# Cross-attention block on one core: the first group's s3, T3 and s2 on VectorE, T2's own sums in the first group's last product

## The chip, the cores and the metric

One core of a Trainium2 chip runs the whole block in one launch. The time is device microseconds (us) of that core. A profile is one execution recorded by the hardware profiler; its engines are PE (TensorE's matmuls; PEld its weight loads), DVE (VectorE), ACT (ScalarE), POOL (GpSimd) and SP (SyncE, which here only issues DMAs). PE, DVE, ACT, POOL and SP each work through a queue of their own in order and wait for each other through semaphores.

## The reference

Everything is float32. With x of 8 x 256 tokens by 512, and as many tokens of context:

```python
q = layer_norm(x, ln1_w, ln1_b) @ q_w + q_b          # 16 heads of 32
k, v = ctx @ k_w + k_b, ctx @ v_w + v_b
out = softmax(mask(q @ k.T / sqrt(32))) @ v
hidden = out @ cproj_w + cproj_b + x
y = gelu(layer_norm(hidden, ln2_w, ln2_b) @ fc_w + fc_b)   # 512 -> 2048
return hidden + y @ proj_w + proj_b                        # 2048 -> 512
```

## The kernel before

The 2048 tokens are four groups (`g` = 0 to 3) of 512. Attention comes first for all groups; the change lies behind it, in the loop over `g` from line 1194, which does fc, gelu and proj for one group at a time. At its start all operands of fc lie in SBUF or in DRAM; `proj_w` is loaded during group 0.

Matrix products are made by the Winograd form of Strassen's scheme: both operands are cut into quarters "11", "12", "21", "22", and seven products of sums of quarters stand in for eight. The table `B_SUMS` (line 209) gives the right operand's sums, t1 = 12 - 11, t2 = 22 - t1, 12 = 22 - 12 (in place), t4 = 21 - t2; `A_SUMS` the left operand's s1 to s4.

**fc.** `product(k, ...)` for k = 0 to 6 makes the seven products of the outer level. Each is again cut into seven, the calls of `sub`, so a product is 7 x 8 = 56 matmul records and a group's fc is 392. `sub(n, ...)` writes PSUM bank n. The order within one product is: bank 1, copied by ACT to u1; bank 6, which DVE adds to u1, giving u2; bank 7, added to u2, giving u3; bank 5 ("22"); then bank 1 is added to a second time, then bank 7 a second time, then bank 5's second tile. So u3 must have been read from bank 7 before PE writes there again, five `sub`s into the product, and the next product's third `sub` needs bank 7 empty. DVE empties banks by adds with one operand in PSUM; GpSimd, which here works on SBUF only, adds the results into the blocks of `h`. In products 3 and 4 DVE also takes pieces of the next group's layer norm statistics (`norm_piece`), and at the start of each product, in group 1 alone, pieces of `proj_w`'s own sums (`some_p2`, lines 1318, 1319). A product ends by issuing the load of its weights for the next group (`load_w2`) on SP.

**gelu.** ACT applies it to the blocks of `h`; those of "21" and "22" during product 6, those of "12" behind it.

**proj, outer level.** `proj_w`'s quarters lie in `pw`; four sums are made from them in place in group 0 by the generator `sum_pw` on DVE, four pieces each, in this order: T3 (in "12"), T2 ("t2"), T1 ("t1"), T4 ("t4"). `some_pw(4)` makes one such sum; the four calls stand at lines 1368, 1484, 1507 and 1545. On the other side `sum_h` makes s3 = 11 - 21, s2 = 22 - s3 (in "21"), s1 = 21 + 11 (in "11") and s4 = 12 - 21 (in "12"), again four pieces each; in group 0 all of them on GpSimd, in the later groups s3, s2 and s1 on DVE and s4 on GpSimd (`deep` is true from group 1 on). In group 0 `proj(bank, a, w, ...)` issues 32 matmul records a time, in the order 11 x 11 (bank 1, which DVE then reads into u1 with `proj_b` added), s3 x T3 (bank 7), 12 x 21 (added to bank 1), s2 x T2 (bank 6), s1 x T1 (bank 5), s4 x 22, 22 x T4 (added to bank 7). Between them PE transposes the next group's tokens (`turn_next`), and DVE and GpSimd add the results and the bias (`bias_ht`, two adds on GpSimd) to the tile `ht`. Behind the last but one product DVE makes the sums of the next group's y (`y_sums`, then `split_y`), which the next group's product 0 reads.

**proj, inner level.** From group 1 on, four of these seven products (12 x 21, s2 x T2, s1 x T1, s4 x 22) are cut once more (`deep_proj`). That needs `B_SUMS` of the weights "21", T2, T1 and "22" themselves, four pieces each (`p2_sums`): three results lie in one of two places of the tile `p2` (place 0 for T2 and "22", place 3 for T1 and "21"), the third sum goes in place into `pw`, and behind the fourth piece SP stores the place to DRAM (`p2_dram`, 768 KB). T1's are made in group 0. The others are made in group 1: "22" on DVE in products 0 to 2, "21" on GpSimd, two pieces behind product 1 and two behind product 2, and T2's on DVE in products 4 to 6, over "22". From then on `p2_load` brings each back from DRAM before it is used; the order of use in a group is "21", T2, T1, "22".

Of the kernel before, what the change touches and what calls it, by code (L numbers as in the profile page):

```python
# [22 lines left out]
def tile_xattn_block(  # L23
# [299 lines left out]
    with ExitStack() as att:  # L323
# [460 lines left out]
        V, GP = nc.vector, nc.gpsimd  # L784
# [175 lines left out]
        g = 1  # L960
        begin(g, 6, 1, load_res, 0, *QUARTERS)
        begin(g, 7, 1, bias_res, 0)
        g = 2
# [6 lines left out]
        g = NG - 1  # L970
# [24 lines left out]
        def run(pieces):  # L995
            for p in pieces:
                p()
# [25 lines left out]
        k, q, v, tx = project_qk(0, "kT"), project_qk(0, "qT"), project_v(0), turn_x(0)  # L1023
# [77 lines left out]
    with ExitStack() as mlp:  # L1101
# [68 lines left out]
        def p2_sums(n, eng=V):  # L1170
            x = pw_blocks(n)
            for i in range(4):
                sum_up(eng, x, B_SUMS, i)
                if i == 3:
                    nc.sync.dma_start(p2_dram[n], p2_place(n))
                yield

        p2_late = {n: p2_sums(n, e) for n, e in (("22", V), ("21", GP), ("t2", V))}

        def some_p2(n, pieces):  # L1180
            for _ in zip(range(pieces), p2_late[n]):
                pass

        def p2_load(n):
            nc.sync.dma_start(p2_place(n), p2_dram[n])

        def some_pw(n):
            for f in zip(range(n), pw_sums):
                pass
# [4 lines left out]
        for g in range(NG):  # L1194
# [18 lines left out]
            def sum_h(which, q, eng=GP):  # L1213

                x = {n: h[n][:, :, 2 * q : 2 * q + 2, :] for n in h}
                to, a, b, op = {
                    "s3": ("s3", "11", "21", ALU.subtract),
                    "s2": ("21", "22", "s3", ALU.subtract),
                    "s1": ("11", "21", "11", ALU.add),
                    "s4": ("12", "12", "21", ALU.subtract),  # L1220
                }[which]
                add(eng, x[to], x[a], x[b], op)
# [7 lines left out]
            def norm_piece():  # L1230

                if g + 1 < NG:
                    if not norm:
                        norm.append(layer_norm(hids[g + 1], f"m{g + 1}", nc.scalar))
                        seen, roots, _ = norm[0]
                        norm.extend([*seen, *roots])
                    norm.pop(1)()
# [6 lines left out]
            def bias_ht():  # L1244

                for b, bias in ((0, projb[:, :HD2]), (1, pbd)):
                    o = out_quarter(b, 0)
                    add(GP, o, o, by_tiles(bias))
# [24 lines left out]
            def product(k, *sums):  # L1273


                wt, yn = w2[g, k], QI[FC_ORDER[k][1]]
                bank = {}

                def y_of(n):
                    if n in QUARTERS:  # L1280
                        return ys[g].t[:, yn, int(n[0]) - 1, ts(int(n[1]) - 1, P)]
                    return y2s[g][:, ("t1", "t2", "t4").index(n), yn, :]

                def sub(n, w, b, first, last):
                    if first:
                        bank[n] = bank_of(n, f"pf{n}_{k}").rearrange("p i (j s) -> p (i j) s", j=2)
                    for m in range(HF // 2):
                        mm(
                            bank[n][:, m, :],
                            wt[:, QI[w], ts(m, P)],  # L1290
                            y_of(b),
                            first and m == 0,
                            last,
                        )

                def u(n):
                    return us(n, f"u{n}_{k}").rearrange("p i (j s) -> p (i j) s", j=2)

                def made(cd, n, x):
                    some_gelus()  # L1300
                    if k in (3, 4) and cd != "22":
                        norm_piece()
                    if sums[0][1] is None:
                        add(V, block(sums[0][0], cd), bank[n], x)
                        return

                    r = h["s3"][:, parts[0] % 4 // 2, parts[0] % 2 * HF // 2 :][:, : HF // 2]
                    parts[0] += 1
                    add(V, r, bank[n], x)
                    for to, base in sums:  # L1310
                        add(GP, block(to, cd), block(base, cd), r)

                sub(1, "11", "11", True, False)
                u1 = u(1)
                nc.scalar.copy(u1, bank[1])  # L1315
                if g == 1:

                    some_p2("22", (2, 1, 1, 0, 0, 0, 0)[k])
                    some_p2("t2", (0, 0, 0, 0, 1, 1, 2)[k])
                sub(6, "s2", "t2", True, True)  # L1320
                u2 = u(2)
                add(V, u2, bank[6], u1)
                some_gelus()
                sub(7, "s3", "12", True, False)
                u3 = u(3)
                add(V, u3, bank[7], u2)
                some_gelus()
                sub(5, "21", "t1", True, False)
                made("22", 5, u3)
                sub(1, "12", "21", False, True)  # L1330
                some_gelus()
                for to, base in sums:
                    if base:
                        add(V, block(to, "11"), bank[1], block(base, "11"))
                    else:
                        nc.scalar.copy(block(to, "11"), bank[1])
                sub(7, "22", "t4", False, True)
                made("21", 7, u2)
                sub(5, "s4", "22", False, True)
                made("12", 5, u2)  # L1340
                load_w2(w2_place[g, k])
# [3 lines left out]
            load_next()  # L1345
            product(1, ("11", "21"))
            if g == 1:
                some_p2("21", 2)
            gelu("11", 0)
            ht = residual(work, hid_dram[g], "resm", f"resm_{g}")  # L1350
            product(2, ("21", "21"))
            if g == 1:
                some_p2("21", 2)
            product(3, ("12", "21"))
            if g == 0:
                load_pw("11", "12", "22")
# [3 lines left out]
            if g == 0:  # L1360
                load_pw("21")
            product(5, ("21", "21"))
            norm_piece()
            gelu("21", 0)
            gelu("22", 1)
            product(6, ("12", "12"))
            norm_piece()
            some_pw(4)
            some_gelus(len(gelus))
            gelu("12", 1)  # L1370
            deep = g > 0
            for which in ("s3", "s2"):
                for q in range(NQF):
                    sum_h(which, q, V if deep else GP)
            if not deep:
                bias_ht()

            bank = {n: bank_of(n, f"py{n}") for n in ((1, 7) if deep else (1, 7, 6, 5))}

# [25 lines left out]
            def o_add(eng, b, k, x):  # L1405
                o = out_quarter(b, k)
                add(eng, o, x, o)
# [93 lines left out]
                sum_h("s4", q)  # L1501
            if deep:
                o_add(GP, 0, 0, as_tiles(hsum[:, 4]))
                bias_ht()
            turn_next(2)
            turn_next(3)
            some_pw(4)
# [20 lines left out]
            if deep:  # L1528
                x_s4, pieces = h_blocks("12", hsum[:, 0], hsum[:, 1], hsum[:, 3])
                run(pieces[:1])  # L1530
                deep_proj(
                    x_s1, "t1", free(3), pieces[1:2], pieces[2:3], pieces[3:], y_sums[:1], y_sums[1:2]
                )
                if g + 1 < NG:
                    p2_load("21")
                for b in range(2):
                    o_add(GP, b, 1, as_tiles(free(3)))
                add_us()
                deep_proj(x_s4, "22", free(0), (), (), y_sums[2:3], y_sums[3:])
                if g + 1 < NG:  # L1540
                    p2_load("t2")
                o_add(V if g + 1 == NG else GP, 0, 1, as_tiles(free(0)))
            else:
                add_us()
                some_pw(4)
                proj(bank[5], "11", "t1", True, True)
                o_add(V, 0, 1, bank[5])
                o_add(V, 1, 1, bank[5])
                for _ in p2_sums("t1"):
                    pass  # L1550
                run(y_sums)
                bank[3] = bank_of(1, "py3")
                proj(bank[3], "12", "22", True, True)
                o_add(V, 0, 1, bank[3])
            store(0)
            if g + 1 < NG:
                y2 = wpool.tile([P, 3, 7, P], F32, tag="y2", bufs=1, name=f"y2_{g + 1}")
                split_y(g + 1, y2, 0, 1, 2, 3)
                proj(bank[7], "22", "t4", False, True)
                o_add(V, 1, 0, bank[7])  # L1560
                store(1)
            else:

                store(1, slice(HD2, D))
                for i in range(2):
                    proj(bank[7], "22", "t4", False, True, (i,))
                    o = ht[:, 2 + i, :HD2]
                    add(V, o, last_7[1] if i else bank[7][:, 0, :], o)
                    store(1, slice(HD2), (i,))
# [41 lines left out]
```

## Time and profile before

| | |
|---|---|
| median of 3 runs (lowest, highest) | 722.44 us (722.06, 723.33) |
| profiled execution, its span | 723.32 us, 721.5 us |
| granted TensorE clock | 1.00 throughout |
| PE busy | 712.7 us (99%) |
| DVE busy | 504.9 us (70%) |
| POOL busy | 486.1 us (67%) |
| ACT busy | 327.8 us (45%) |
| mean DMA rate over the span | 208 GB/s |

PE's records can be read as stages: its first fc matmul of group 0 starts at 348.53 us, group 0's proj at 392.31, group 1's fc at 442.98 and its proj at 489.07, group 2's fc at 536.55 and its proj at 580.33, group 3's fc at 627.81. The rest, up to 348.53, is the attention part. Matmuls are pipelined, so a row's length includes the tail of its last matmul, and the pace is read from start to start.

### The profile page before, as it was taken

The numbers are of one execution on the slowest core, as the hardware profiler recorded it, in microseconds if no ns is written. First come the engines' busy times: TensorE is split into PE (matmuls) and PEld (weight loads), VectorE is DVE, ScalarE is ACT, GpSimd is POOL, SyncE is SP. The second block draws the span as 40 slices with busy tenths as digits, with TensorE's granted clock in tenths as the row PEclk, the third lists the DMA queues.
The fourth block names the chain that finished last, engine by engine and source line by source line (L and its number), as shares of the span: only waits on it lengthen the run. The fifth ranks groups of instructions, "written<-read, shape, count | busy, mean of one in ns | idle before, by whom it ended". The sixth has DMA issues, their size and how long they took to land.

```text
span 721.5 us, 14867 instructions
## 1 busy us (share of the span) xinstructions
PE 712.7 (99%) x5397; PEld 630.9 (87%) x5397; DVE 504.9 (70%) x1204; ACT 327.8 (45%) x928; POOL 486.1 (67%) x430
## 2 busy tenths in 40 slices
PE   8999999999999999999999999999999999999998
PEld 7878877877887777777999889988999999999997
DVE  3676765674557556887678597799776897766972
ACT  2267788766866787872034300217103072030500
POOL 3758799987786999886559960882554835547253
PEclk9999999999999999999999999999999999999999
DMA  9516646687739785942699603995248942475021
GB/s 292 193 60 182 246 157 224 195 310 264 230 118 291 270 267 201 380 131 87 216 404 371 235 1 113 378 372 203 88 147 327 326 178 89 145 264 204 2 88 59
DMA packets 77401, 149.90 MB, mean 208 GB/s; under 512 B 7140, under 2 KB 45328, under 8 KB 74640
## 3 DMA queue, kind: packets, MB, share of 16 engines
q1 hardware_dynamic: 77072, 148.92, 58.7%
q8 instruction: 43, 0.70, 0.4%
q14 instruction: 30, 0.25, 0.1%
q0 software_dynamic: 256, 0.02, 0.0%
HBM read 112.22 MB, written 36.70 MB: 206 GB/s over the span
## 4 chain that ended last, share of the span: by engine, by line
PE 87%; DVE 3%; DMA 2%; ACT 2%; POOL 2%; issue 2%; SPq 0%; DVEq 0%; ACTq 0%; POOLq 0%
PE pf L1119 18%; PE py L1119 12%; PE ppt L699 8%; PE pv L441 7%; PE pqT L441 7%; PE po L441 6%; PE pd_t L1119 5%; PE pd L1119 5%; PE pkT L441 5%; PE s L646 5%; PE av L715 5%; PE pkT L538 2%; POOL h L1122 2%; ACT h L1259 2%; DMA pw<-in_L_xattn_proj_w_dram 2%
## 5 line engine op out<-in xcount | busy, mean ns | idle before, releaser
L1119 PE MATMUL pf<-y,w 128*128 128x128 f32 x1568 | 176.5, 276 | 1.5 <-DVE u L1122 1.5
L1119 PEld LDWEIGHTS pf<-y,w 128*128 128x128 f32 x1568 | 175.9, 192 | 2.3 <-DVE u L1122 2.1
L1122 POOL TENSOR_TENSOR h<-h,hs 128x512 f32<-128x512 f32 x88 | 113.7, 1314 | 89.4 <-DVE hs L1122 88.8
L688 POOL TENSOR_TENSOR pr<-pr,rsum 128x512 f32<-128x512 f32 x128 | 129.5, 1044 | 36.0 <-DVE rsum L686 23.8
L674 ACT ACTIVATE pr<-pr,nmax 128x256 f32<-128x256 f32 x256 | 127.7, 502 | 35.3 <-DVE nmax L664 35.2
L664 DVE CUSTOM_DVE_ANT_0 pr<-s,mb 128x256 f32<-128x256 f32 x256 | 93.6, 413 | 39.7 <-PE s L646 28.0
L1315 ACT COPY u<-pf 128x512 f32<-128x512 f32 x28 | 16.4, 585 | 164.8 <-PE pf L1119 164.8
L699 PEld LDWEIGHTS ppt<-ident,pr 128*128 128x128 f32 x512 | 57.3, 140 | 14.9 <-issue 5.2
L699 PE MATMUL ppt<-ident,pr 128*128 128x128 f32 x512 | 68.8, 277 | 0.3
L1122 DVE TENSOR_TENSOR hs<-pf,u 128x512 f32<-128x512 f32 x72 | 49.5, 688 | 12.4 <-PE pf L1119 10.8
L1259 ACT ACTIVATE h<-h,cols 128x256 f32<-128x256 f32 x128 | 52.0, 494 | 12.0 <-POOL h L1122 12.0
L1122 POOL TENSOR_TENSOR h<-h,h 128x512 f32<-128x512 f32 x20 | 27.5, 1398 | 42.9 <-DVE hs L1122 13.4
L1122 DVE TENSOR_TENSOR u<-pf,u 128x512 f32<-128x512 f32 x56 | 38.7, 690 | 25.0 <-PE pf L1119 21.3
L704 ACT COPY pt<-ppt 128x512 f32<-128x512 f32 x96 | 51.8, 573 | 7.1 <-PE ppt L699 7.1
L441 PE MATMUL pv<-vw,ctxT 128*128 128x256 f32 x224 | 52.4, 381 | 0.0
L441 PE MATMUL pqT<-xnT,qw 128*128 128x256 f32 x224 | 51.0, 380 | 0.0
L674 ACT ACTIVATION_READ_ACCUMULATOR pr<-pr,nmax 128x1 f32 x256 | 48.8, 190 | 0.0
L441 PEld LDWEIGHTS pqT<-xnT,qw 128*128 128x128 f32 x224 | 41.5, 191 | 4.9
L441 PEld LDWEIGHTS pv<-vw,ctxT 128*128 128x128 f32 x224 | 41.1, 191 | 5.3 <-issue 0.3
L1119 PE MATMUL py<-pw,h 128*128 128x256 f32 x192 | 42.4, 380 | 0.0
L1119 PE MATMUL py<-pw_t,h 128*128 128x256 f32 x192 | 42.3, 380 | 0.0
L1119 PEld LDWEIGHTS py<-pw_t,h 128*128 128x128 f32 x192 | 36.2, 190 | 4.7
(212 smaller groups left out, 1292.1 us busy)
## 6 DMA issues: line engine op xcount, KB each, us to landing
w<-w_dram SPq DMA_DIRECT2D x16, 1792.0 KB, 9.3
w<-in_L_xattn_fc_w_dram SPq DMA_DIRECT2D x36, 256.0 KB, 6.3
w<-w_dram SPq DMA_DIRECT2D x12, 768.0 KB, 7.6
ctx<-in_ctx_dram SPq DMA_DIRECT2D x16, 256.0 KB, 4.9
x<-in_x_dram SPq DMA_DIRECT2D x16, 256.0 KB, 4.5
v_dram<-st_v SPq DMA_DIRECT2D x16, 256.0 KB, 2.2
v<-v_dram SPq DMA_DIRECT2D x16, 256.0 KB, 4.6
resx<-in_x_dram SPq DMA_DIRECT2D x16, 256.0 KB, 4.6
```

The costliest lines, as they stand in the source:

```text
L441: nc.tensor.matmul(bank[n][:, i, :], l[:, c, ts(i, P)], r[:, c, :], start=first and i == 0 and c == 0, stop=last and c == HC - 1, skip_gro ...
L646: nc.tensor.matmul(banks[j][:, i, :], qT[j * HD : (j + 1) * HD, b * S + i * P : b * S + (i + 1) * P], kT[j * HD : (j + 1) * HD, b * SK : ( ...
L664: nc.vector.tensor_tensor_reduce(pr[:, j, i, :], banks[j][:, i, :], mbias[g][1][:, b, :], scale=-SCALE, scalar=FLT_MAX, op0=ALU.add, op1=A ...
L674: nc.scalar.activation(pr[:, j, i, :], pr[:, j, i, :], AF.Exp, bias=nmax[:, j, i : i + 1], scale=-1.0, accum_out=sums[:, j, i : i + 1],)
L688: nc.gpsimd.tensor_tensor(pr[:, j], pr[:, j], rsum[:, j, :, None].to_broadcast([P, NQ, SK]), ALU.mult,)
L699: nc.tensor.transpose(ps[:, kc, ts(i, P)], probs[n][:, j, i, ts(kc, P)], ident)
L704: nc.scalar.copy(pt, ps)
L715: nc.tensor.matmul(av[j * HD : (j + 1) * HD, :], vs[g, hg][:, b * NK + kc, ts(j, HD)], pts[n, j][:, kc, :], start=(kc == 0), stop=(kc == N ...
L1119: nc.tensor.matmul(ps, lhsT, rhs, start=first, stop=last, skip_group_check=True)
L1122: eng.tensor_tensor(to, a, b, op)
L1259: nc.scalar.activation(h[n][:, :, p, :], h[n][:, :, p, :], AF.Gelu_apprx_tanh, bias=col(c_fcb, half * HF + p), scale=1.0,)
L1315: nc.scalar.copy(u1, bank[1])
```

## The change

In group 0, s3 and s2 are made by VectorE like those of the later groups, and T3 is made between the two, where it was ahead of both. The bias adds of group 0 on GpSimd move from in front of the first product of proj to behind s4, where they are in the other groups.

T2's own sums are made in group 0, on VectorE, between `split_y` and the last product, and stored to DRAM; the next group's y sums go ahead of T1's own sums there. In group 1, VectorE makes the own sums of "21", one piece in each of products 0 to 3, and GpSimd those of "22", at the points where it made those of "21". Behind product 5 SP issues the load of T2's own sums from DRAM over "22".

```diff
-        p2_late = {n: p2_sums(n, e) for n, e in (("22", V), ("21", GP), ("t2", V))}
+        p2_late = {n: p2_sums(n, e) for n, e in (("21", V), ("22", GP))}
...
                 if g == 1:
-
-                    some_p2("22", (2, 1, 1, 0, 0, 0, 0)[k])
-                    some_p2("t2", (0, 0, 0, 0, 1, 1, 2)[k])
+                    some_p2("21", (1, 1, 1, 1, 0, 0, 0)[k])
                 sub(6, "s2", "t2", True, True)
...
             product(1, ("11", "21"))
             if g == 1:
-                some_p2("21", 2)
+                some_p2("22", 2)
...
             product(2, ("21", "21"))
             if g == 1:
-                some_p2("21", 2)
+                some_p2("22", 2)
...
             product(5, ("21", "21"))
+            if g == 1:
+                p2_load("t2")
             norm_piece()
             gelu("21", 0)
             gelu("22", 1)
             product(6, ("12", "12"))
             norm_piece()
-            some_pw(4)
             some_gelus(len(gelus))
             gelu("12", 1)
             deep = g > 0
             for which in ("s3", "s2"):
                 for q in range(NQF):
-                    sum_h(which, q, V if deep else GP)
-            if not deep:
-                bias_ht()
+                    sum_h(which, q, V)
+                if which == "s3":
+                    some_pw(4)
...
             if deep:
                 o_add(GP, 0, 0, as_tiles(hsum[:, 4]))
-                bias_ht()
+            bias_ht()
...
                 o_add(V, 1, 1, bank[5])
+                run(y_sums)
                 for _ in p2_sums("t1"):
                     pass
-                run(y_sums)
...
                 split_y(g + 1, y2, 0, 1, 2, 3)
+                if not deep:
+                    for _ in p2_sums("t2"):
+                        pass
                 proj(bank[7], "22", "t4", False, True)
```

## The prediction

> **What bounds the kernel.** The page's first table gives PE 99% of the span, so I looked only for PE's losses. The table of busy time by stage comes first, cut at PE's own borders: the fc products of groups 1 and 2 (numbers from zero), which issue the same 392 matmuls.
>
> ```profile
> 442.98:489.07 46.09, 44.56 (x393) 43.99 (x392) 38.61 (x58) 10.16 (x22) 31.33 (x25) 1.00 0.85 317
> 536.55:580.33 43.78, 43.78 (x394) 43.77 (x392) 31.44 (x50) 10.57 (x23) 25.00 (x21) 1.00 0.83 303
> ```
>
> The first number is the length: 46.09 against 43.78, at the same clock of 1.00, so group 1 loses 2.31 us. Group 2 needs exactly 392 x 0.1117 us. PE's timeline says where:
>
> ```profile
> 399.21 2.75 PE L1119 MATMUL py<-pw,hs 128*128 128x256 f32 x12
> 402.27 4.58 PE L1119 MATMUL py<-pw,hs 128*128 128x256 f32 x20 [0.30 <-POOL hs L1122]
> 406.69 1.04 PE L274 MATMUL pyt<-ident,hm 128*128 128x128 f32 x8
> 442.98 29.64 PE L1119 MATMUL pf<-y,w 128*128 128x128 f32 x264
> 473.31 6.52 PE L1119 MATMUL pf<-y,w 128*128 128x128 f32 x56 [0.70 <-DVE u L1122]
> 480.14 6.52 PE L1119 MATMUL pf<-y,w 128*128 128x128 f32 x56 [0.31 <-DVE u L1122]
> 487.18 2.05 PE L1119 MATMUL pf<-y,w 128*128 128x128 f32 x16 [0.52 <-DVE u L1122]
> ```
>
> Rows: start, length, engine, count, and in brackets the idle time and its releaser. Group 1 stops once in each of products 4, 5 and 6 (a product is 6.25 us, so product 4 starts at 468.0), always for a VectorE add that empties a bank. Group 0 stops once: 399.21 to 406.69 is 7.48 us for 32 matmuls that take 6.90 elsewhere (392.31 to 399.21), a loss of 0.58. **Together 2.89 us can be had**, and nothing else near the change costs PE time.
>
> **Why VectorE is late in group 1.** Its timeline in products 4 to 6, only the lines of T2's own sums and the bank adds behind them:
>
> ```profile
> 470.25 1.61 DVE L219 TENSOR_TENSOR p<-pw_t 128x512 f32<-128x512 f32 x1 [0.35 <-DMA p_dram<-p]
> 471.79 1.47 DVE L1122 TENSOR_TENSOR u<-pf,u 128x512 f32<-128x512 f32 x2
> 478.01 0.68 DVE L219 TENSOR_TENSOR p<-pw_t,p 128x512 f32<-128x512 f32 x1
> 482.91 1.15 DVE L219 TENSOR_TENSOR pw_t<-pw_t 128x512 f32<-128x512 f32 x1
> 483.98 1.75 DVE L219 TENSOR_TENSOR p<-pw_t,p 128x512 f32<-128x512 f32 x1
> ```
>
> The first even waits for the store of "22" to leave the same place. Then u2 and u3 run at 471.79 to 473.26, and PE needs bank 7 free at 468.0 + 5 x 0.893 = 472.5. The four cost 0.68 to 1.75 us each, short alone and long beside GpSimd.
>
> **Part 1: T2's sums leave products 4 to 6.** What is left there on VectorE is what group 2 has, which loses nothing. Gain 2.31. Bounds: GpSimd's backlog from its four sums could keep part of it; it stands idle 2.91 us before its run of nine adds at 474.23, so it has caught up, and I take the whole. If not, at worst nothing comes (rival B).
>
> **Part 2: the first group's s3, T3, s2 on VectorE.** Now GpSimd makes s3 beside T3 on VectorE, and both are slowed. Group 2 shows the same s3 and s2 on VectorE:
>
> ```profile
> 393.67 5.72 DVE L1122 TENSOR_TENSOR pw<-pw,pw 128x512 f32<-128x512 f32 x4
> 400.02 6.09 DVE L1122 TENSOR_TENSOR pw_t<-pw,pw 128x512 f32<-128x512 f32 x4
> 395.44 6.78 POOL L1122 TENSOR_TENSOR hs<-h,h 128x512 f32<-128x512 f32 x4
> 402.18 6.29 POOL L1122 TENSOR_TENSOR h<-h,hs 128x512 f32<-128x512 f32 x4
> 581.79 3.55 DVE L1122 TENSOR_TENSOR hs<-h,h 128x512 f32<-128x512 f32 x4
> 585.26 2.49 DVE L1122 TENSOR_TENSOR h<-h,hs 128x512 f32<-128x512 f32 x4
> ```
>
> VectorE is free at 393.75, when the gelus of "21" (8 x 0.404 us from 389.72) are done. s3: 3.55, plus 0.54 because GpSimd's last adds overlap it to 395.48 here and only 1.19 us there: 4.1 (at most T3's 5.72). T3: GpSimd has nothing to run before s2's first piece, so 2.49 (at most 5.72). It ends at 400.3; PE wants its last piece at 399.21 + 12 x 0.2156 = 401.8. The 0.58 stall goes; at both upper ends T3 would end at 405.2 and PE lose 3.4.
>
> s2 follows: one piece 0.62, then three beside GpSimd's s1, which s2 releases, at T2's 6.09 / 4 = 1.52: 5.2 (0.62 to 1.75 a piece: 2.5 to 5.9). Behind it waits u1, 0.69, now 406.2 in place of 400.1. PE needs u1 before it adds to bank 1 again, at 407.56 - 0.58 = 407.0: cover 0.8, at the upper end 0.1. T2's pieces (needed at 414.8) start after 406.2 and end by 412.3. GpSimd's s1 and s4 move ahead by some 4 us; the two bias adds (1.26 each) go behind s4, before the adds of u2 and u3 at 423.23, where GpSimd now waits 0.70. Cost nothing; without that cover they would delay those adds by 2.5.
>
> A rule that speaks against this: the Trainium skill, "SBUF — State Buffer", section "Who interferes with whom", says that a VectorE operation with two SBUF inputs and a GpSimd one that reads SBUF exclude each other for a whole instruction. By that rule each shared piece costs an estimated 0.62 + 1.26 = 1.88, u1 ends at 407.3, and the time would be about 0.3 longer, 719.9. The rows above agree that both suffer but stay under it (1.43 to 1.70).
>
> **Part 3: T2's sums in group 0's last product.** VectorE's lines there:
>
> ```profile
> 433.17 2.69 DVE L219 TENSOR_TENSOR y<-y 128x512 f32<-128x512 f32 x4
> 440.01 1.08 DVE L307 TENSOR_TENSOR y<-y,y 128x896 f32<-128x896 f32 x1
> 443.25 0.69 DVE L1122 TENSOR_TENSOR resm<-py,resm 128x512 f32<-128x512 f32 x1 [2.15 <-PE py L1119]
> ```
>
> The 2.15 us of idle time ahead of the last add is the room. T1's four sums took 430.64 to 433.17, 2.53, with GpSimd idle, as it is here (nothing after 427.85). All 0.58 earlier: split_y ends at 440.5, the sums at 443.05 (7.0 if each took 1.75: 447.5), the add 0.69 later at 443.75. Product 0 wants its bank 7 two subproducts in, at 442.40 + 1.79 = 444.2. Cover 0.45, so I cost it nothing; at the upper end 4.0.
>
> **Part 4: queues.** VectorE's "21" takes the places of "22" in products 0 to 2 (one piece less in product 0), and one piece in product 3, where VectorE waits 1.09 us for PE: even at 1.75 u3 ends at 465.8, PE needs it at 466.2. GpSimd's four sums only change their block. On SP T2's store moves from 485.76 to about 443, ahead of group 0's last output stores and of the weight load at 449.4, which wait for later events; T1's store moves from 433.28 to 435.3. "21"'s first sum at 443.8 overwrites T1's place: that store landed in 3.2 us, so 438.5 (the slowest such store took 12.8: 448.1, and PE would lose 3.0). GpSimd's first sum (457.9) overwrites T2's place: landed by 446 to 456. The added reload, 768 KB, goes out near 483, behind product 5's weights; such reloads land in 4.2 to 4.5 us, and T2 is used at 510.89 - 2.89 = 508. Hidden, with over 10 us to spare even at 12.8.
>
> **Sum.** The profiled execution took 723.32 (span 721.54, 1.8 around it), 0.88 above the median of the three runs. 723.32 - 2.31 - 0.58 = 720.43 for it; taken off the median, 722.44 - 2.89 = **719.55**. The three runs spread from -0.38 to +0.89, so the case's own range is 718.9 to 720.4.
>
> **Rivals.** A: u1 is late in group 0 (pieces of s2 at 1.75 or more, or GpSimd's adds dragging on), and the 0.58 is spent again: 720.1. For: cover of 0.8 only. Against: no row of four shared pieces averages over 1.52 on VectorE. Chance 0.07.
>
> B: PE's stops in products 4 to 6 stay, since others (GpSimd, the statistics pieces) hold VectorE back; only 0.58 comes: 721.9. Against: group 2 has all of these and none of the stops. Chance 0.12, T1's late store and a part of the stops moved to product 3 counted here, since they end in the same place.
>
> C, slower: all twelve pieces from s3 to s2 run at T3's present 1.43, because VectorE is what slows itself there. 393.75 + 17.2 + 0.69 = 411.6 against 407.0: PE loses 4.6, 724.2. It decides from a mean piece of 1.29 on, where the loss of 2.9 eats the gain; I count on (4.1 + 2.49 + 5.2) / 12 = 0.98. For: T3's own row. Against: GpSimd's s3 beside it is the work that goes. Chance 0.08.
>
> My forecast has 0.73. A measurement of this kernel can tell about 0.2% (1.4 us) from no change: forecast and A are faster (0.80), B the same (0.12), C slower (0.08). The range reaches towards B: 718.9 to 721.4.
>
> **What would show it.** Group 1's fc stage at 43.8 us, group 0 from 392.31 to its end at 50.1, no stop of PE between; T3 at some 2.5 us; u1 before 407; the last add of group 0 right behind T2's sums. Wrong if PE stops at bank 1 near 407, at bank 7 near 444, or in products 0 to 3 of group 1.

## The result, and the profile after

Six runs of the kernel after gave a median of 719.55 us (719.12 to 720.14), six of the kernel before on the same chip 722.22 (722.06 to 723.33): a ratio of 0.9961, interval 0.9949 to 0.9974, so 1.9 to 3.7 us faster. 719.55 had been forecast.

The stages of PE in the kernel after, group 0's proj and group 1's fc (start and end, length, then busy time and count of instructions of PE, PEld, DVE, ACT and POOL, clock, DMA share, GB/s):

```profile
391.31:441.41 50.10, 50.10 (x242) 44.23 (x241) 42.56 (x50) 12.69 (x26) 23.68 (x15) 1.00 0.38 145
441.41:485.18 43.77, 43.77 (x393) 43.77 (x392) 35.57 (x56) 10.56 (x23) 30.68 (x25) 1.00 0.91 349
```

They took 50.67 and 46.09 before: 0.57 and 2.32 shorter, the two amounts of the forecast (0.58 and 2.31). PE's timeline no longer has a break in either; s3 x T3 and all of group 1's fc are one row each:

```profile
398.22 7.07 PE L1119 MATMUL py<-pw,hs 128*128 128x256 f32 x32
441.41 43.93 PE L1119 MATMUL pf<-y,w 128*128 128x128 f32 x392
```

VectorE behind product 6 of group 0, with GpSimd's s1 (start, length, engine, count):

```profile
392.76 3.55 DVE L1122 TENSOR_TENSOR hs<-h,h 128x512 f32<-128x512 f32 x4
396.24 2.48 DVE L1122 TENSOR_TENSOR pw<-pw,pw 128x512 f32<-128x512 f32 x4
398.65 2.48 DVE L1122 TENSOR_TENSOR h<-h,hs 128x512 f32<-128x512 f32 x4
401.06 0.68 DVE L1122 TENSOR_TENSOR v<-py,projb 128x512 f32<-128x512 f32 x1
399.47 7.83 POOL L1122 TENSOR_TENSOR h<-h,h 128x512 f32<-128x512 f32 x4 [5.51 <-DVE h L1122]
```

T3 went from 5.72 to 2.48 us. s2 was not slowed by s1 at all; here it is GpSimd that pays, 1.96 a piece. And the end of group 0's last product, T2's own sums (first and last), the add that frees bank 7, and the first sum of "21":

```profile
439.45 0.68 DVE L219 TENSOR_TENSOR p<-pw_t 128x512 f32<-128x512 f32 x1
441.37 0.69 DVE L219 TENSOR_TENSOR p<-pw_t,p 128x512 f32<-128x512 f32 x1
441.97 0.69 DVE L1122 TENSOR_TENSOR resm<-py,resm 128x512 f32<-128x512 f32 x1
442.58 0.68 DVE L219 TENSOR_TENSOR p<-pw 128x512 f32<-128x512 f32 x1
```

Bank 7 is free at 442.66; PE wants it at 441.41 + 1.79 = 443.20, so 0.54 us are left.

The two profiled executions stand further apart than the medians: 723.32 and 719.35, 3.97 us. 2.89 of that is the two stages. Another 1.13 lies ahead of all of this: group 0's fc began at 348.53 before and at 347.40 after. PE waited 1.34 us for the first weights of k in the one and not at all in the other, but that can't be the whole reason: the second profile of the kernel before (below) waited 0.21 there and still began at 348.42. In the eleven further profiles of before and of variants that could be cut into stages, that part, which no variant touches, ended between 347.1 and 349.1 us. Single times of this kernel therefore scatter by some 2 us, and the experiments are read by the length of the stages first. One run (four more sums, below) left only the profile of a disturbed execution, which can't be cut into these stages, and was made a second time.

### The profile page after: what moved, and what is told of

Same layout as the page of the kernel before. It is cut to its first block, busy times and chain, and to the rows that moved or that the text cites. A ratio compares the mean times of both kernels' runs of the same rounds, so it can differ in the third digit from the quotient of the medians.

```text
span 717.6 us, 14855 instructions
## 1 busy us (share of the span) xinstructions
PE 711.9 (99%) x5397; PEld 630.3 (88%) x5397; DVE 506.7 (71%) x1212; ACT 327.7 (46%) x928; POOL 473.8 (66%) x422
## 4 chain that ended last, share of the span: by engine, by line
PE 94%; DVE 2%; ACT 2%; POOL 1%; issue 1%; DVEq 0%; POOLq 0%
PE pf L1119 22%; PE py L1119 13%; PE ppt L699 8%; PE pv L441 7%; PE pqT L441 7%; PE po L441 6%; PE pd_t L1119 5%; PE pd L1119 5%; PE pkT L441 5%; PE s L646 5%; PE av L715 5%; PE pkT L538 2%; POOL h L1122 1%; ACT h L1259 1%; PE pxt L274 1%
## 5 line engine op out<-in xcount | busy, mean ns | idle before, releaser
L1122 POOL TENSOR_TENSOR h<-h,hs 128x512 f32<-128x512 f32 x84 | 105.9, 1283 | 88.0 <-DVE hs L1122 87.8
```

The source lines that it names most:

```text
L1122: eng.tensor_tensor(to, a, b, op)
```

## The experiments

**The two halves alone.** First the kernel before with part 2 only:

```diff
-            some_pw(4)
...
-                    sum_h(which, q, V if deep else GP)
-            if not deep:
-                bias_ht()
+                    sum_h(which, q, V)
+                if which == "s3":
+                    some_pw(4)
...
-                bias_ht()
+            bias_ht()
```

> The kernel before with part 2 alone: s3, T3, s2 on VectorE in group 0 and the bias adds behind s4; T2's own sums stay in products 4 to 6 of group 1. Two stages are read from PE's starts: group 0's proj (50.67 us before, 50.10 after) and group 1's fc (46.09 before, 43.77 after). My theory, that the two gains have separate causes: proj 50.1, fc 46.1, time 722.2 - 0.57 = 721.6. Rival, that group 0's change also feeds group 1's gain through VectorE and GpSimd being ahead: fc below 45.5, time below 721.1.

Then the kernel after with just these lines undone.

> The kernel after with part 2 undone: T2's own sums in group 0's last product, the rest of group 0 as before. My theory: proj 50.67, fc 43.8, time 722.2 - 2.3 = 719.9. Rival, that group 1's stops go only because GpSimd and VectorE enter it freer: fc stays above 45, time above 721. A second rival: without the freed GpSimd, T2's sums make the seam late and PE stops at bank 7 at the start of group 1: fc 44.3 or more.

| | proj of group 0 | fc of group 1 | median, and of before on that chip | ratio (interval) |
|---|---|---|---|---|
| part 2 alone | 50.11 | 44.85 | 721.52, 722.14 | 0.9995 (0.9983 to 1.0007) |
| T2's sums moved alone | 50.66 | 43.78 | 720.91, 722.14 | 0.9978 (0.9969 to 0.9988) |

Group 0's 0.57 belongs to part 2 and to nothing else. Without T2's sums in products 4 to 6, fc is free of stops whatever group 0 does. But part 2 alone left fc at 44.85, not 46.1, which is the mark of the rival, and its one break there with a wait behind it is of another kind. This is its timeline of PE, and the issues of SP at 460.4 us in it, then at 460.4 in the kernel after (count, KB, us to landing):

```profile
473.31 13.12 PE L1119 MATMUL pf<-y,w 128*128 128x128 f32 x112 [0.46 <-DMA w<-w_dram]
```

```profile
w<-w_dram SPq DMA_DIRECT2D x1, 1792.0 KB, 12.9
```

```profile
w<-w_dram SPq DMA_DIRECT2D x1, 1792.0 KB, 9.9
```

The load issued at 460.37 holds product 5's weights: 460.37 + 12.9 = 473.27, and PE starts product 5 at 473.31, 0.62 later than its pace; the other 0.46 of the 1.08 that this stage is over 43.77 came in product 6, behind VectorE. So two questions were open: how much of the 2.31 is VectorE's time, and what delays these weights.

**T2's sums in products 4 to 6 without a store in their way.**

```diff
-        p2_late = {n: p2_sums(n, e) for n, e in (("21", V), ("22", GP))}
+        p2_late = {n: p2_sums(n, e) for n, e in (("t2", V), ("21", GP))}
...
-                    some_p2("21", (1, 1, 1, 1, 0, 0, 0)[k])
+                    some_p2("t2", (0, 0, 0, 0, 1, 1, 2)[k])
...
-                some_p2("22", 2)
+                some_p2("21", 2)
...
-            if g == 1:
-                p2_load("t2")
...
-                    for _ in p2_sums("t2"):
+                    for _ in p2_sums("22"):
```

> The kernel after, but the own sums that are made in group 0's last product are those of 22, not T2's; T2's are back on VectorE in products 4 to 6 of group 1, 21's on GpSimd as before, nothing on VectorE in products 0 to 3. So the first of T2's sums no longer waits for a store to leave its place (0.35 us before). My theory, that VectorE's time on the four sums makes its bank adds late: fc 45.6 to 46.1, time 721.4 to 721.9. Rival, that the wait for the store started the lateness and VectorE never caught up: fc 43.8 to 44.3, time 719.6 to 720.1.

fc took 44.85, between the two: neither theory alone. Median 721.04 against 722.14, ratio 0.9982 (0.9972 to 0.9991). One stop is left, in product 6. **The kernel before, profiled again:**

> The kernel before once more, for a second profile. If the 1.2 us of group 1's loss that T2's sums alone did not show hangs on the store of 22 landing a few tenths before or after VectorE's first T2 sum, the fc stage of group 1 lies between 44.8 and 46.1 and changes with that wait; if all of it is VectorE's own time, it is 46.1 again.

This execution of the very same kernel took 44.90 for that stage, and 50.67 for group 0's proj as the first did; its time was 722.00. The landing of the store of "22" in the first profile and in this one, then this one's PE rows of group 1's fc and VectorE's T2 sums of products 4 and 6, with the bank adds behind them:

```profile
p_dram<-p SPq DMA_DIRECT2D x1, 768.0 KB, 12.8
```

```profile
p_dram<-p SPq DMA_DIRECT2D x1, 768.0 KB, 12.5
```

```profile
442.86 42.48 PE L1119 MATMUL pf<-y,w 128*128 128x128 f32 x376
485.87 2.05 PE L1119 MATMUL pf<-y,w 128*128 128x128 f32 x16 [0.54 <-DVE u L1122]
```

```profile
469.85 0.69 DVE L219 TENSOR_TENSOR p<-pw_t 128x512 f32<-128x512 f32 x1
470.46 1.48 DVE L1122 TENSOR_TENSOR u<-pf,u 128x512 f32<-128x512 f32 x2
...
481.58 1.16 DVE L219 TENSOR_TENSOR pw_t<-pw_t 128x512 f32<-128x512 f32 x1
482.66 1.75 DVE L219 TENSOR_TENSOR p<-pw_t,p 128x512 f32<-128x512 f32 x1
484.34 1.48 DVE L1122 TENSOR_TENSOR u<-pf,u 128x512 f32<-128x512 f32 x2
```

Here the store of "22" landed 12.5 us after its issue in place of 12.8, the first sum began 0.07 us behind the operation ahead of it and ran in 0.69 in place of 1.61, and the bank adds behind it were in time. 1.13 of loss is left: 0.8 in product 6, whose two sums run beside GpSimd and take 2.8 us, the rest in slips of a tenth or two ahead of it. So some 1.1 us are VectorE's time on the sums. The other 1.2 stand in the first profile alone, where the first sum came 0.35 later for the store and took 0.92 longer. VectorE's own schedule says the same: u2 of product 6 begins 42.68 us into the stage in the first profile, and 41.43 to 41.48 in this one, with part 2 alone and with "22" made early, whatever PE lost on the way. The kernel before itself thus meets the mark of part 2's rival (fc below 45.5), so group 0's change need not feed group 1's stage.

**The store and product 5's weights.** In the kernel after, the stores of "21" and "22" go out together at 466.2 us; before, that of "22" went out at 457.4, ahead of those weights. This variant brings one back:

```diff
-                    some_p2("21", (1, 1, 1, 1, 0, 0, 0)[k])
+                    some_p2("21", (2, 1, 1, 0, 0, 0, 0)[k])
```

> The kernel after with the own sums of 21 on VectorE two, one, one in products 0 to 2, like those of 22 before, so that their store goes out near 456 us, ahead of the weight load for product 5, in place of 466. In the kernels with a store there (before, s3 only) that load took 12.6 and 12.9 us, in the others 9.9 to 10.2. My theory, that this store is what delays the weights: the load takes 12.5 or more and PE stops for 0.3 to 0.6 at the start of product 5, fc 44.1 to 44.4, time 719.9 to 720.1. Rival, that the weights were late for another reason: load 10, fc 43.8.

The store went out at 456.49 and the weights, issued at 461.02, took 12.4 us: 473.42, where product 5 is due at 442.07 + 31.27 = 473.34. fc took 43.98, 0.21 longer, all of it at the start of product 5 (473.44): the mechanism as expected, the size below it. Median 720.07 against 722.68, ratio 0.9968 (0.9957 to 0.9980), no clear difference from the kernel after. In both profiles of the kernel before the same load took 12.3 and 12.6 us, so in the second of them the weights came at 474.1, just as product 5 was due, and in the first at 474.5, 0.3 late, hidden only by VectorE's lateness. The change removed a second limit that PE had never been seen to wait for.

**The order in group 0.** T3 behind s2, or ahead of s3:

```diff
                 for q in range(NQF):
                     sum_h(which, q, V)
-                if which == "s3":
-                    some_pw(4)
+            some_pw(4)
```

> The kernel after with T3 behind s2 in place of between s3 and s2. My theory, that PE waits for each piece of T3: the first piece ends at 396.24 + 4 x 0.62 + 0.62 = 399.3 us on the time axis of the kernel after, PE wants it at 398.22, so PE loses 1.1: proj 51.2, time 719.55 + 1.1 = 720.7. Rival, that VectorE is far enough ahead for any order of the three: proj 50.1, time 719.55.

```diff
+            some_pw(4)
             for which in ("s3", "s2"):
                 for q in range(NQF):
                     sum_h(which, q, V)
-                if which == "s3":
-                    some_pw(4)
```

> The kernel after with T3 ahead of s3, so the order is T3, s3, s2. My theory, that only the engine matters between these two orders: T3 takes 3.1 to 3.6 beside GpSimd's last adds, s3 2.5, its last piece done by 398.9 and wanted at 400.8; proj 50.1, time 719.55. Rival, that T3 runs at its rate of before (1.43 a piece) since its operands slow it: T3 ends at 398.5, s3's first piece at 399.1 against 398.22: proj 51.0, time 720.4.

T3 first: T3 took 3.56 us, as expected, and proj 50.10; median 719.19 against 722.70, ratio 0.9947 (0.9930 to 0.9963); the place of T3 ahead of s2 is what counts, not the one between. T3 last: 57.38, median 727.78 against 722.14, ratio 1.0077 (1.0062 to 1.0092), over six times the loss that I had worked out. Its timeline, and its stages by clock (the last number but two, 0.86, 0.50 and so on, is the granted clock):

```profile
398.48 6.60 POOL L1122 TENSOR_TENSOR h<-h,h 128x512 f32<-128x512 f32 x4 [3.10 <-DVE h L1122]
402.21 4.62 DVE L1122 TENSOR_TENSOR pw<-pw,pw 128x512 f32<-128x512 f32 x4
404.06 9.93 PE L1119 MATMUL py<-pw,hs 128*128 128x256 f32 x32 [4.26 <-issue]
```

```profile
399.64:404.06 4.42, 0.16 (x2) 0.03 (x1) 4.42 (x4) 3.03 (x5) 4.42 (x4) 0.86 1.08 424
404.06:409.00 4.94, 4.94 (x12) 3.83 (x13) 4.94 (x7) 0.00 (x0) 1.02 (x1) 0.50 0.70 295
409.00:410.00 1.00, 1.00 (x5) 0.81 (x4) 0.84 (x2) 0.00 (x0) 0.00 (x0) 0.66 0.00 0
410.00:413.82 3.82, 3.82 (x19) 3.31 (x18) 0.00 (x0) 0.00 (x0) 0.00 (x0) 1.00 0.02 4
```

s2's first piece releases GpSimd's s1, and soon four pieces on VectorE, s2's last two and T3's first two, take turns with GpSimd's, 1.68 us from start to start (398.86, 400.54, 402.21, 403.88). T3's first piece came so late that PE stood for 4.42 us; and then the clock fell to 0.50 for 5.6 us (404.06 to about 409.7), so the 32 matmuls took 9.76 in place of 6.91. 4.42 + 2.85 = 7.27 is the whole loss of 7.28.

**The bias adds in group 0**, back ahead of proj's first product:

```diff
                 if which == "s3":
                     some_pw(4)
+            if not deep:
+                bias_ht()
...
-            bias_ht()
+            if deep:
+                bias_ht()
```

> The kernel after with the bias adds of group 0 back ahead of proj's first product on GpSimd, so GpSimd works beside VectorE's s3. My theory, that the moved bias costs and brings nothing: s3 up to 1.6 us longer, T3's last piece by 400.4 against 400.8 wanted, proj 50.1, time 719.55. Rival (C of the prediction, a mean piece of 1.29 or more whenever GpSimd has work): proj 51 or more, time 720.5 or more.

Proj took 51.14, 1.04 longer; median 721.29 against 722.70, ratio 0.9975 (0.9964 to 0.9986). The rows of s3, the bias adds, T3 and PE's s3 x T3 in it:

```profile
392.61 5.71 DVE L1122 TENSOR_TENSOR hs<-h,h 128x512 f32<-128x512 f32 x4
393.76 1.73 POOL L1122 TENSOR_TENSOR resm<-resm,projb 128x512 f32<-128x512 f32 x1
395.45 1.72 POOL L1122 TENSOR_TENSOR resm<-resm,pbd 128x512 f32<-128x512 f32 x1
...
398.24 2.48 DVE L1122 TENSOR_TENSOR pw<-pw,pw 128x512 f32<-128x512 f32 x4
399.02 7.15 PE L1119 MATMUL py<-pw,hs 128*128 128x256 f32 x32 [0.80 <-PE py L1119]
```

s3 is 2.16 longer. T3 ends at 400.7, and its last piece alone, wanted at 400.65, would cost nothing to speak of. Its first piece does: it is done at 398.9, and PE wants it at 398.06. My expectation had looked at the last piece alone. With the bias adds left in place, part 2 would have cost 0.47 (51.14 against 50.67) in place of bringing 0.57: the line that seemed to be tidying up decides the sign.

**The room in group 0's last product.**

```diff
                 if not deep:
+                    for _ in range(4):
+                        sum_up(V, pw_blocks("t2"), B_SUMS, 0)
                     for _ in p2_sums("t2"):
```

> The kernel after with the first of T2's own sums made four times more (the same values again) in group 0's last product, ahead of T2's sums: 4 x 0.62 = 2.5 us more on VectorE. My theory, that the seam has a cover of 443.20 - 442.66 = 0.54 us and VectorE sets it: bank 7 comes 1.9 to 2.0 late, fc of group 1 45.7, time 721.5. Rival, that the room in the last product is larger than the rows show (PE's wish for bank 7 could be met otherwise): fc 43.8, time 719.55.

> The kernel after with the first of T2's own sums made four times more in group 0's last product, once more for its profile. My theory as before: bank 7 is late by 4 x 0.62 - 0.54 = 1.9, fc of group 1 45.7. Rival, since its median was 4 us above that of the kernel after: the lateness runs on into product 0's own adds and the stage is 47 or more.

Medians 723.79 against 722.70, ratio 1.0009 (0.9999 to 1.0020), and 723.33 against 722.68, ratio 1.0010 (0.9998 to 1.0023). In the second's profile:

```profile
439.00 3.59 DVE L219 TENSOR_TENSOR p<-pw_t 128x512 f32<-128x512 f32 x5
...
444.44 0.68 DVE L1122 TENSOR_TENSOR resm<-py,resm 128x512 f32<-128x512 f32 x1
```

```profile
445.17 42.25 PE L1119 MATMUL pf<-y,w 128*128 128x128 f32 x376 [2.26 <-DVE resm L1122]
```

Five sums into one place take 0.73 each, so the four added 2.9, not 2.5; less the cover of 0.54 that is 2.4, and fc took 46.29, 2.52 longer. The stop is one, at bank 7, and nothing of it runs on into product 0. The cover is real and small. The medians lie some 1.3 us above what this stage accounts for, and the clock on record with each time offers a cause. The profiled execution, 721.45, and the next fastest, 722.05, had a mean granted clock of 1.000; the other six, 723.02 to 724.27, had 0.998, and so had six of the nine times of the first run that lie below 725. Among the times below 730 us no other kernel has less than 0.999, but for the one with T3 last (0.995). 0.002 of 720 us is an estimated 2.9 us at half the clock, which costs PE some 1.4. So the stop of 2.26 us seems to halve the clock behind it in most executions, as the longer one with T3 last does. No trace of such an execution is at hand; this is argued, not shown.

**The last group's stop**, which both kernels have (PE waits 0.25 us for the blocks of 12). First those blocks ahead of all of s1:

```diff
+            if g + 1 == NG:
+                t = rows_of(place("h12_own", w2_place[g, 4]).t)
+                own = [t[:, i].rearrange("p (c s) -> p c s", c=HF // 2) for i in range(4)]
+                x_12, pieces = h_blocks("12", *own)
+                run(pieces)
             for q in range(NQF):
                 sum_h("s1", q, V if deep else GP)
...
-                x_12, pieces = h_blocks("12", *own)
-                run(pieces)
+                if g + 1 < NG:
+                    x_12, pieces = h_blocks("12", *(free(i) for i in range(4)))
+                    run(pieces)
```

> The kernel after with one more edit, in the last group alone: VectorE makes the blocks of 12 (h_own), which PE waits for there, ahead of s1, which is used much later. My theory: that stop (0.25 us idle, 0.41 of pace) goes, the last group from the start of its proj to the end takes 49.5 in place of 49.9, time 719.1. Rival, that GpSimd or the gelus set those blocks: 49.9, time 719.55.

Then s1's pieces between the bank adds of the first inner product:

```diff
-            for q in range(NQF):
-                sum_h("s1", q, V if deep else GP)
+            s1 = [lambda q=q: sum_h("s1", q, V if deep else GP) for q in range(NQF)]
+            if g + 1 < NG:
+                run(s1)
...
-                deep_proj(x_12, "21", hsum[:, 4])
+                deep_proj(x_12, "21", hsum[:, 4], *([f] for f in s1 if g + 1 == NG))
```

> The kernel after, in the last group alone: the blocks of 12 (h_own) directly behind those of s2, and s1's four pieces one by one between the bank adds of the first inner product (12 x 21), where VectorE waits for PE. In the run that put all of s1 in one row there, the bank adds behind it came late (0.76 us idle for PE). My theory: neither stop, last proj stage 46.0 in place of 46.41, time 0.4 below the kernel after: 719.1. Rival, that the pieces between the adds run beside GpSimd and delay them: 46.4 or more.

Both moved the stop and did not remove it: the stage, to PE's last matmul, took 46.93 and 46.35 in place of 46.41, neither near the 46.0 hoped for. In the first, s1 ran 4.64 us in one row beside GpSimd and the bank adds behind it were late (0.76 us idle for PE); in the second a stop of 0.20 turned up in the product behind. Medians 720.00 against 722.70 (ratio 0.9958, 0.9944 to 0.9973) and 719.26 against 722.68 (0.9966, 0.9953 to 0.9980): nothing that beats the kernel after.

## Why the prediction was right, and where it was not

**The place of the gain** was right. PE's losses, in group 0's proj and in group 1's fc, their releasers and their removal came as told, and nothing new took their place.

**Part 1's 2.31** is the term that was mis-sized. It was taken as VectorE's time on four sums. Some 1.1 us of it are that, product 6's pair beside GpSimd above all; 1.2 hung on the 0.35 us wait for the store of "22", which the second profile of the kernel before did not have. From the stages the change is worth 0.57 + 1.13 = 1.7 us against that second execution and 2.9 against the first. How often the kernel before loses the 1.2 was not settled, and the medians point both ways: on the first chip the whole change gave 2.67 (interval from 1.9), and T3 first on another 3.5 (from 2.7), which fits only the larger amount; on the chip of the first four experiments part 2 alone gave 0.62 (up to 1.2) and T2's sums alone 1.23 (up to 2.24), which fits only the smaller (the larger would make them 1.81 and 2.32). The wait was in the prediction, as a remark beside the sum; it should have been a term with two ends. That the figure met the median to the hundredth is luck. The reading "short alone and long beside GpSimd" did not hold either: the sum at 478.01 took 0.68 in the middle of GpSimd's nine adds, and there it was GpSimd's add, begun at 478.07, that took 1.75.

**Part 2.** T3 at 2.49: measured 2.48. s3 at 4.1: 3.55, since GpSimd's last adds overlapped it for 1.20 us, as in group 2, and not for 0.54 more. s2 at 5.2: 2.48, so u1 was done 4.3 us before PE needed it (401.74 against 406.00), not 0.8; rival A had no ground in this order. It would have had in another: with T3 last, s2's last two pieces do take turns with s1. T3 was checked by its last piece; its first had the smaller cover, 1.3 us (396.92 against 398.22), and is the one that both runs with a loss there ran into. "Cost nothing" for the bias adds was right as a cost, and missed that the move is what makes part 2 a gain.

Of the rule weighed there, from the Trainium skill's "SBUF — State Buffer", "Who interferes with whom", the runs show this much: two engines at this work do take turns piece by piece, 1.68 us a pair with T3 last, below the estimate of 1.88, and a row of VectorE's pieces can also pass at 0.62 while GpSimd's piece is held (in the kernel after, s1's first piece, begun at 399.47, took 2.80 us). s2's row took 2.48 or 2.49 in all nine profiles with T3 ahead of it and 4.63 in the one with T3 behind it, with s1 released by s2's first piece every time; what decides which of the two happens, no run here shows.

**Part 3.** T2's four sums 2.52 (2.53 told), cover at bank 7 0.54 (0.45 told).

**Part 4.** T1's store landed in 3.3 us (3.2 told). "21"'s piece in product 3 took 1.52 and u3 was in time. The reload, issued at 481.47, took 9.3 us in place of 4.2 to 4.5 and was still 16 us early (T2 is used at 507.0). The order of the stores on SP, told as harmless, was better than that: product 5's weights land 2.4 to 2.7 us sooner in the stage.

**Rivals B and C.** B expected the stops to have other causes; 43.78 with T2's sums moved alone excludes it, though the weights that it did not name were next in line. C's mechanism, VectorE slowing itself, is excluded by 2.48 for T3 with GpSimd idle; its 1.43 a piece is what s3 took with the bias adds beside it (5.71 for four).

## What to carry to other kernels

A stop in one profile may belong to that execution: a wait of tenths of a microsecond for a DMA, ahead of a chain without slack, wants a second profile of the same kernel before its whole consequence is booked as a gain. Where an engine works through a row of pieces that another consumes in order, check when the first piece is due, not only the last, and see what else is released beside it. Before an edit is called neutral because its engine is idle, look at what the other engines do beside it while it is idle: here VectorE's s3 took 3.55 us, and 5.71 with GpSimd at work.

## What was not expected of the hardware

- A stop of 4.42 us cost 2.85 us more, since the granted clock was 0.50 for the next 5.6 us; one of 2.26 us idle (four more sums) left it at 1.00 in the execution that was profiled, but most executions of that kernel show 0.998 over their whole length, in place of 0.999 to 1.000. Behind PE's last matmul of an execution the clock fell after 2.3 to 5.1 us in the thirteen profiles. The Trainium skill, "TensorE: Matmul & The Clock Gate", "Part 1: The HAM clock gate", has the half clock after an idle window of some 3.4 us, which agrees with the stop of 4.42, and its end after about as much sustained work, which here took 5.6.
- A 768 KB store issued 4.5 us ahead of a 1792 KB load on SP lengthened that load: 12.3 to 12.9 us in the four profiles with such a store (twice the kernel before, part 2 alone, "21" sooner), 9.6 to 10.8 in the nine without.
